# Which queue issues the loads, and when a step turns its tiles: a transformer block on one Trainium2 core

## The chip, the cores and the metric

The kernel runs on one core of one Trainium2 chip. The metric is the device time of one execution in microseconds (us), lower is better. The core has TensorE (PE in the profile: matmuls; PEld: its weight loads), VectorE (DVE), ScalarE (ACT), GpSimd (POOL) and SyncE (SP). Each engine works through its own instruction stream in the order of the program and waits on semaphores. Transfers are issued by an instruction in the stream of SP, ACT or POOL; they are then carried out by 16 DMA engines.

## The reference, cut to what matters

A parallel transformer block over 4 sequences of 512 tokens with 512 features, all in float32: layer norm, causal attention with 16 heads and ALiBi slopes, and a gated feed-forward part whose three 2048 x 512 weight matrices are cubic splines through a few thousand control points.

```python
x = L0_attn_x                                   # (4, 512, 512)
xn = _layernorm(x, axis=-1)
# attention, 16 heads of 32
scores = einsum('bhqd,bhkd->bhqk', q, k) / sqrt(32) + slope[h] * distance[k]
attn = softmax(where(causal, scores, min), axis=-1)
ctx = einsum('bhqk,bhkd->bhqd', attn, v)
# feed-forward, weights interpolated from control points
inter = silu(xn @ gate_w.T) * (xn @ up_w.T)
x = x + ctx @ Wo + bo + inter @ down_w.T
```

## The kernel before, in words

There are two stages. In the first (attention) the normalised x of each batch is turned, projected to q, k and v, and run through softmax; the second (feed-forward) works on few interpolated rows instead of the dense weights. The change lies wholly in the first.

**Units and steps.** Attention is cut into 64 units: 4 batches (b), 4 groups of 4 heads (hg), and 4 query tiles of 128 queries in the order i = 0, 3, 2, 1 (`QUERIES`). Unit i has (i+1)*128 keys. A loop over n issues in step n parts of several units, so each engine's stream is a fixed software pipeline. Before the change, step n issues in this order:

- `swap(n-2)`: DVE turns the unit's probabilities in 32 x 32 blocks (L896, waits for POOL), then SP issues four transfers (L898) that gather the blocks into `moved` (i = 1 to 3, one buffer) or `first` (i = 0);
- `normalize(n-1)`: DVE takes reciprocals of the sums (L878, waits for ACT), POOL multiplies (L880);
- `scores(n)`: PE multiplies q and k into four PSUM banks `s` (L840), DVE adds the ALiBi distance, takes the minimum of the negated score and writes `p` (L851, four instructions, called the minima here);
- `values` in every fourth step (n = 4g+7, for group g): PE multiplies probabilities and v (L914), ACT keeps the result (L929);
- `exponentials(n)`: ACT (L866);
- the spline terms: DVE multiplies and adds tables (L1034) that become the feed-forward weights. A credit decides how many a step gets: `TERMS[n % 4]` is added, each term has a cost. When a term has read its buffer, the next load into that buffer is issued in the same step;
- `items[n]` and `small[n]`: projections (L777, L813), the output projection (L484, with the addition on DVE at L491 and its write `mid` at L494), statistics, and loads.

A unit's `p{i}` has one buffer. So the minima of unit n+4, which has the same i, wait until the four transfers of unit n have read it. `moved` has one buffer too, so the transfers of i = 3 wait until the previous group's `values` have read it. The four `s` banks make `scores(n+1)` wait for the minima of unit n.

**Queues.** Nearly all transfers are issued by SP, in program order with the four of each swap: loads of x (`load_x`, L595), of the tables for the spline terms (L645, L646, L671), of xT for the residual (`proj`'s `load`, L479), of features (`load_feat`, L548), and writes of samples (`keep_samples`, L499 to L503) and moments (`stretch_moments`, L527). POOL issues the copies into `table` (L545).

Of the kernel before, what the change touches and what calls it, by code (L numbers as in the profile page):

```python
# [18 lines left out]
P = 128  # L19
# [4 lines left out]
NB = D // P  # L24
# [5 lines left out]
LAG_SWAP = 2  # L30
# [21 lines left out]

TERMS = (1.4, 0.7, 1.4, 0.7)
NW, NW4 = 11, 4
# [346 lines left out]
def block_kernel(  # L401
# [70 lines left out]

    def proj(b, r, pool, tag):

        xt = []

        def load():
            xt.append(xtp.tile([P, S], F32, name="xt"))
            nc.sync.dma_start(out=xt[0], in_=xT[b, r * P : (r + 1) * P, :])  # L479

        def go():
            ps = pool.tile([P, S], F32, name=tag)
            for c in range(NB):
                nc.tensor.matmul(  # L484
                    ps,
                    lhsT=wsb["o"][:, c, r * P : (r + 1) * P],
                    rhs=ctxT[b][:, c, :],
                    start=(c == 0),
                    stop=(c == NB - 1),
                )  # L490
            nc.vector.scalar_tensor_tensor(  # L491
                xt[0], ps, bocol[:, r : r + 1], xt[0], ALU.add, ALU.add
            )
            nc.sync.dma_start(out=mid[b][:, r], in_=xt[0])  # L494

        return [load, go]

    def keep_samples(b):
        nc.sync.dma_start(  # L499
            out=samples[b][1 : D + 1].rearrange("(c p) s -> p c s", p=P), in_=xnT[b]  # L500
        )
        nc.sync.dma_start(out=samples[b][:1], in_=lone[0][:1])
        nc.sync.dma_start(out=samples[b][D + 1 : D + NW], in_=lone[0][: NW - 1])  # L503

    def stretch_moments(b, pool):
# [15 lines left out]
        for k, ps in enumerate(banks):  # L521
            n = 64 if k == 2 else P
            o = pool.tile([P, S], F32, name="out", bufs=3)
            nc.scalar.copy(o[:n], ps[:n])
            for s, (at, half) in place.items():
                if at == k:
                    nc.sync.dma_start(out=rows[s], in_=o[half * 64 : (half + 1) * 64])  # L527

# [17 lines left out]

    def load_feat(b, q):
        nc.sync.dma_start(out=feat[b][:, q], in_=table[b][:, q])  # L548

# [27 lines left out]
    with ExitStack() as att:  # L577
# [11 lines left out]

        def load_x(b, tiles=range(NB)):  # L590
            if tiles[0] == 0:
                xpt[b] = xpp.tile([P, NB, D], F32, name="xp")
            for t in tiles:
                r = (b * NB + t) * P
                nc.sync.dma_start(out=xpt[b][:, t], in_=xpf[r : r + P, :])  # L595

# [39 lines left out]
        def row_terms():  # L636
# [4 lines left out]

            def load(n):
                c, w = parts[n]
                tab, own = place(n % 2)
                nc.sync.dma_start(out=tab, in_=coef[c])  # L645
                nc.sync.dma_start(out=own, in_=rowpts[c, w])  # L646

            for n, (c, w) in enumerate(parts):
# [6 lines left out]
                if c:  # L655
                    terms.append((1.2, to, to, tmp, ALU.add))
            return [lambda: load(0), lambda: load(1)]

        def down_terms():
# [7 lines left out]
            def load(*steps):  # L667
                for n in steps:
                    for k, source in enumerate((downtab, downpts)):
                        given = source[at[n] : at[n + 1]].rearrange("(p x) -> p x", p=P)  # L670
                        nc.sync.dma_start(out=part(n, k), in_=given)  # L671

            loads[len(terms) - 1] = lambda: load(0, 1, 2)
            for n, (kind, lo, hi, c) in enumerate(DOWN_STEPS):
                to = (dR if kind == "v" else dM)[:, lo:hi].rearrange("p a n -> p (a n)")
# [263 lines left out]
        def project_out(b, spots):  # L939
            for r, n in enumerate(spots):  # L940
                load, go = proj(b, r, ps_m, "mm")
                items[n - 2].append(load)
                items[n].append(go)

        for b in range(B):
# [16 lines left out]
            if b + 1 < B:  # L962
# [8 lines left out]
                if b + 2 < B:  # L971
                    items[at + 11].append(lambda b=b: load_x(b + 2))
        for b in range(B):
# [4 lines left out]
        for q in range(NB):  # L978
            items[54 + NB * q].append(lambda q=q: load_feat(0, q))
        for b in range(B):  # L980
# [30 lines left out]
        for load in first_loads:  # L1011
            load()
        done, credit = 0, 0.0

        for n in range(len(units) + LAG):
            u = units[n] if n < len(units) else None
            if 0 <= n - LAG_SWAP < len(units):
                swap(units[n - LAG_SWAP])
            if 0 <= n - 1 < len(units):
                normalize(units[n - 1])  # L1020
            if u:
                scores(u)
# [248 lines left out]
```

## Time and profile before

| | |
|---|---|
| median of three runs | 556.83 us (554.96 to 560.12) |
| profiled execution, its own time | 559.8 us |
| its span, first to last instruction | 558.0 us |
| mean granted TensorE clock | 0.959 |
| PE busy | 521.5 us, 93% |
| DVE busy | 370.1 us, 66% |
| ACT busy | 259.1 us, 46% |
| POOL busy | 241.3 us, 43% |
| q1 (transfers issued by SP) | 107.78 MB, 65.4% of 16 engines' span |
| q0 (transfers issued by POOL) | 8.40 MB, 5.3% |

The steps of the first stage run from about 25 us to 398 us; the feed-forward stage takes the rest. A busy share of PE counts matmuls with ends that the profile models, so a matmul that is stretched by a wait or by a lower clock counts as busy. The durations below are therefore held against the shortest ones of the same shape. ACT issues no transfer in this profile.

### The profile page before, as it was taken

How to read it: one execution, taken by the hardware profiler on the slowest of the kernel's cores; microseconds unless marked ns; L12 is line 12 of the kernel's file. 1: busy time of each engine (PE TensorE's matmuls, PEld its weight loads, DVE VectorE, ACT ScalarE, POOL GpSimd, SP SyncE). 2: the span in 40 equal slices, each digit the busy share in tenths (PEclk: the TensorE clock that was granted, in tenths of full speed). 3: DMA queues.
4: the chain of work that ended last, by engine and by line, in shares of the span. 5: the costliest groups of instructions: out<-in, count | busy, mean ns of one | idle time of the engine just before them, and what ended most of it. 6: DMA issues, size and time to landing. Idle time of an engine off the chain costs nothing.

```text
span 558.0 us, 11701 instructions
## 1 busy us (share of the span) xinstructions
PE 521.5 (93%) x4012; PEld 246.6 (44%) x4012; DVE 370.1 (66%) x934; ACT 259.1 (46%) x710; POOL 241.3 (43%) x428
## 2 busy tenths in 40 slices
PE   7999999699989989998998999986799899999996
PEld 5633443244444433444443434432335555646552
DVE  5177988559688866878985755683143583665836
ACT  2375567256337526633665654655014322534322
POOL 2032545436345643644566445442068476122310
PEclk9999899899989979998999999898799899899999
DMA  8928678987777788776586478687658667645344
GB/s 317 353 89 241 186 224 234 294 215 187 220 231 217 219 279 224 196 226 173 163 240 170 111 224 216 192 242 198 178 173 256 203 228 260 205 149 202 125 160 160
DMA packets 72060, 116.94 MB, mean 210 GB/s; under 512 B 11104, under 2 KB 35680, under 8 KB 71488
## 3 DMA queue, kind: packets, MB, share of 16 engines
q1 hardware_dynamic: 67392, 107.78, 65.4%
q0 software_dynamic: 4608, 8.40, 5.3%
q8 instruction: 32, 0.52, 0.4%
q14 instruction: 28, 0.23, 0.1%
HBM read 49.56 MB, written 23.68 MB: 131 GB/s over the span
## 4 chain that ended last, share of the span: by engine, by line
PE 67%; DMA 12%; issue 6%; SPq 5%; POOL 4%; DVE 4%; ACT 2%; DVEq 0%; POOLq 0%; ACTq 0%
PE mm L777 15%; PE mm L813 8%; PE g L560 7%; PE s L840 7%; PE mm L484 7%; DMA moved<-p 6%; PE c L914 6%; PE o L1147 6%; SPq L898 5%; PE o L1164 3%; PE o L484 3%; PE o L1093 3%; DMA inner<-made 2%; POOL p L880 2%; DVE p L851 2%
## 5 line engine op out<-in xcount | busy, mean ns | idle before, releaser
L880 POOL TENSOR_SCALAR p<-p,inv 128x128 f32<-128x128 f32 (+3 forms) x256 | 147.3, 587 | 206.4 <-DVE inv L878 193.2
L866 ACT ACTIVATE p<-p,low 128x128 f32<-128x128 f32 (+3 forms) x256 | 140.4, 550 | 77.9 <-DVE low L851 41.8
L896 DVE STREAM_TRANSPOSE p<-p 128x512 f32<-128x512 f32 (+1 forms) x64 | 96.2, 1503 | 18.1 <-POOL p L880 18.1
L851 DVE CUSTOM_DVE_ANT_1 p<-s,dist 128x128 f32<-128x128 f32 (+2 forms) x192 | 69.0, 415 | 31.1 <-PE s L840 20.2
L840 PE MATMUL s<-kT,qT 32*128 32x256 f32 (+3 forms) x512 | 72.6, 480 | 8.3 <-DVE low L851 8.2
L1069 POOL COPY made<-inner 128x512 f32<-128x512 f32 x64 | 38.8, 636 | 88.4 <-DVE inner L1068 55.3
L560 PE MATMUL g<-feat,wT 32*64 32x512 f32 x832 | 65.4, 602 | 0.0
L777 PE MATMUL mm<-xnT,wq 128*128 128x512 f32 (+1 forms) x136 | 62.7, 606 | 0.7 <-ACT v L821 0.7
L813 PE MATMUL mm<-wv,xnT 128*128 128x512 f32 x128 | 60.8, 618 | 1.2 <-ACT xnT L762 1.2
L777 PE MATMUL mm<-xnT,wk 128*128 128x512 f32 (+1 forms) x136 | 59.4, 579 | 0.2 <-ACT xnT L762 0.2
L1061 ACT ACTIVATE act<-g 128x512 f32<-128x512 f32 x60 | 31.0, 604 | 59.7 <-PE g L560 59.6
L914 PE MATMUL c<-moved,v 128*32 128x384 f32 (+2 forms) x512 | 42.4, 482 | 16.4 <-DMA moments<-out 7.4
L840 PEld LDWEIGHTS s<-kT,qT 32*128 32x128 f32 x512 | 32.7, 183 | 56.3 <-DVE low L851 26.1
L851 DVE CUSTOM_DVE_ANT_0 p<-s,dist 128x512 f32<-128x512 f32 x64 | 40.3, 686 | 17.6 <-PE s L840 10.9
L866 ACT ACTIVATION_READ_ACCUMULATOR p<-p,low 128x1 f32 x256 | 47.9, 187 | 0.0
L484 PE MATMUL mm<-ctxT,wo 128*128 128x512 f32 x96 | 45.4, 620 | 0.0
L560 PEld LDWEIGHTS g<-feat,wT 32*64 32x64 f32 x832 | 31.3, 136 | 22.2 <-issue 11.7
L1068 DVE TENSOR_TENSOR inner<-g,act 128x512 f32<-128x512 f32 x40 | 24.8, 684 | 22.4 <-PE g L560 10.7
L777 PEld LDWEIGHTS mm<-xnT,wq 128*128 128x128 f32 x136 | 25.8, 198 | 27.8 <-issue 24.7
L777 PEld LDWEIGHTS mm<-xnT,wk 128*128 128x128 f32 x136 | 24.5, 189 | 30.6 <-issue 24.6
L813 PEld LDWEIGHTS mm<-wv,xnT 128*128 128x128 f32 x128 | 23.6, 194 | 31.2 <-issue 25.5
L1147 PE MATMUL o<-inner,dRM 32*64 32x512 f32 x512 | 36.6, 588 | 0.0
(100 smaller groups left out, 575.3 us busy)
## 6 DMA issues: line engine op xcount, KB each, us to landing
moved<-p SPq DMA_DIRECT2D x64, 256.0 KB
moved<-p SPq DMA_DIRECT2D x64, 192.0 KB
moved<-p SPq DMA_DIRECT2D x64, 128.0 KB
feat<-table SPq DMA_DIRECT2D x16, 512.0 KB
inner<-made SPq DMA_DIRECT2D x32, 256.0 KB
table<-samples POOLq DMA_DIRECT2D x64, 88.0 KB, 3.8
xp<-in_xp_dram SPq DMA_DIRECT2D x16, 256.0 KB
feat<-in_coef_dram SPq DMA_DIRECT2D x8, 512.0 KB
```

Of the source, the lines that this page charges most:

```text
L484: nc.tensor.matmul(ps, lhsT=wsb["o"][:, c, r * P : (r + 1) * P], rhs=ctxT[b][:, c, :], start=(c == 0), stop=(c == NB - 1),)
L560: nc.tensor.matmul(ps[k][cols, :], lhsT=wT[rows, q, 2 * w + part, cols], rhs=feat[b][rows, q, part, :], start=(part == 0), stop=(part == 1),)
L777: nc.tensor.matmul(ps[0][:, tokens], lhsT=wsb[name][:, c, hg * P : (hg + 1) * P], rhs=xnT[b][:, c, tokens], start=(c == 0), stop=(c == NB ...
L813: nc.tensor.matmul(ps[0], lhsT=xnT[b][:, c, t * P : (t + 1) * P], rhs=wsb["v"][:, c, :], start=(c == 0), stop=(c == NB - 1),)
L840: nc.tensor.matmul(ps[j], lhsT=qk[b, hg, "q"][rows, i * P : (i + 1) * P], rhs=keys[rows, :, : i + 1], start=True, stop=True,)
L851: nc.vector.tensor_tensor_reduce(out=p[:, :, :, j], in0=ps[j].rearrange("p (r c y) -> p r c y", r=NB, y=Q32), in1=dist[:, :, NB - 1 - i :] ...
L866: nc.scalar.activation(by_head(p)[:, :, j], by_head(p)[:, :, j], AF.Exp, bias=low[:, j : j + 1], scale=-1.0, accum_out=total[:, j : j + 1],)
L880: nc.gpsimd.tensor_scalar(by_head(p)[:, :, j], by_head(p)[:, :, j], inv[:, j : j + 1], 1.0, ALU.mult, ALU.mult)
L896: nc.vector.transpose(flat, flat)
L914: nc.tensor.matmul(ps[j * HD : (j + 1) * HD, i * P : S if i else P], lhsT=vals[b][:, c, hg * P + j * HD : hg * P + (j + 1) * HD], rhs=w[.. ...
L1069: nc.gpsimd.tensor_copy(made[:, k], four[:, k])
L1147: nc.tensor.matmul(sums[b][r][cols, :], lhsT=dR[rows, a, cols], rhs=o[rows, :], start=(a == 0), stop=False,)
```

## The change

It has three parts. First, the loads of x for batches 2 and 3, the table loads that are issued inside the loop, the xT loads of three batches, the feature loads of batch 0, and all writes of samples and moments are issued in ACT's stream. What is issued ahead of the loop stays with SP, as do the transfers of `swap` and the writes of `mid`. Second, a step now issues `scores` first, then `normalize`, `values`, and then `swap`; only the last tile of a group (i = 1) is still turned ahead of the minima. Third, the table loads are issued one step after the term that frees their buffer (`due`), `TERMS` gives 1.6 in place of 1.4 in even steps, and an empty term of cost 2.4 stands ahead of the terms of the down weights.

```diff
-TERMS = (1.4, 0.7, 1.4, 0.7)
+TERMS = (1.6, 0.7, 1.6, 0.7)
...
-    def proj(b, r, pool, tag):
+    def proj(b, r, pool, tag, queue=nc.sync):
...
-            nc.sync.dma_start(out=xt[0], in_=xT[b, r * P : (r + 1) * P, :])
+            queue.dma_start(out=xt[0], in_=xT[b, r * P : (r + 1) * P, :])
...
     def keep_samples(b):
-        nc.sync.dma_start(
+        nc.scalar.dma_start(
             out=samples[b][1 : D + 1].rearrange("(c p) s -> p c s", p=P), in_=xnT[b]
         )
-        nc.sync.dma_start(out=samples[b][:1], in_=lone[0][:1])
-        nc.sync.dma_start(out=samples[b][D + 1 : D + NW], in_=lone[0][: NW - 1])
+        nc.scalar.dma_start(out=samples[b][:1], in_=lone[0][:1])
+        nc.scalar.dma_start(out=samples[b][D + 1 : D + NW], in_=lone[0][: NW - 1])
...
-                    nc.sync.dma_start(out=rows[s], in_=o[half * 64 : (half + 1) * 64])
+                    nc.scalar.dma_start(out=rows[s], in_=o[half * 64 : (half + 1) * 64])
...
-            def load(n):
+            def load(n, queue=nc.scalar):
                 c, w = parts[n]
                 tab, own = place(n % 2)
-                nc.sync.dma_start(out=tab, in_=coef[c])
-                nc.sync.dma_start(out=own, in_=rowpts[c, w])
+                queue.dma_start(out=tab, in_=coef[c])
+                queue.dma_start(out=own, in_=rowpts[c, w])
...
-            return [lambda: load(0), lambda: load(1)]
+            return [lambda: load(0, nc.sync), lambda: load(1, nc.sync)]
...
-                        nc.sync.dma_start(out=part(n, k), in_=given)
+                        nc.scalar.dma_start(out=part(n, k), in_=given)
...
             loads[len(terms) - 1] = lambda: load(0, 1, 2)
+            terms.append((2.4,))
...
-                load, go = proj(b, r, ps_m, "mm")
+                load, go = proj(b, r, ps_m, "mm", nc.scalar)
...
-                    items[at + 11].append(lambda b=b: load_x(b + 2))
+                    items[at + 11].append(lambda b=b: load_x(b + 2, queue=nc.scalar))
...
-            items[54 + NB * q].append(lambda q=q: load_feat(0, q))
+            items[54 + NB * q].append(lambda q=q: load_feat(0, q, nc.scalar))
...
-        done, credit = 0, 0.0
+        done, credit, late = 0, 0.0, []
...
-            if 0 <= n - LAG_SWAP < len(units):
-                swap(units[n - LAG_SWAP])
+            turned = units[n - LAG_SWAP] if 0 <= n - LAG_SWAP < len(units) else None
+            if turned and turned[2] == QUERIES[-1]:
+                swap(turned)
+            if u:
+                scores(u)
             if 0 <= n - 1 < len(units):
                 normalize(units[n - 1])
-            if u:
-                scores(u)
             if n % NB == NB - 1 and n >= NB + LAG:
                 g = n // NB - 1
                 values(g // NHG, g % NHG)()
+            if turned and turned[2] != QUERIES[-1]:
+                swap(turned)
             if u:
                 exponentials(u, range(NG))
...
-            late = []
+            due, late = late, []
             while done < len(terms) and credit > 0.0:
                 cost, *term = terms[done]
-                nc.vector.tensor_tensor(*term)
+                if term:
+                    nc.vector.tensor_tensor(*term)
                 done += 1
                 credit -= cost
                 if done in loads:
                     late.append(loads[done])
-            for step in (*items[n], *small[n], *late):
+            for step in (*items[n], *small[n], *due):
                 step()
```

More of the change, by code (lines that the diff above doesn't have):

```diff
@@ L545, in copy_rows, with load_feat @@
             nc.gpsimd.dma_start(out=to, in_=rows)
-    def load_feat(b, q):
-        nc.sync.dma_start(out=feat[b][:, q], in_=table[b][:, q])
+    def load_feat(b, q, queue=nc.sync):
+        queue.dma_start(out=feat[b][:, q], in_=table[b][:, q])
     def product(b, q, w, pool, tag):
@@ L588, in block_kernel, with load_x @@
         xpt = {}
-        def load_x(b, tiles=range(NB)):
+        def load_x(b, tiles=range(NB), queue=nc.sync):
             if tiles[0] == 0:
@@ L594, in load_x @@
                 r = (b * NB + t) * P
-                nc.sync.dma_start(out=xpt[b][:, t], in_=xpf[r : r + P, :])
+                queue.dma_start(out=xpt[b][:, t], in_=xpf[r : r + P, :])
         for k in range(2):
```

## The prediction, made before the changed kernel ran

> **What bounds the kernel now.** I read the page first, then busy time by stretches, the timeline of one engine at a time inside the stretches where PE idles, and the waits of DVE. The page:
>
> ```profile
> span 558.0 us, 11701 instructions
> PE 521.5 (93%) x4012; PEld 246.6 (44%) x4012; DVE 370.1 (66%) x934; ACT 259.1 (46%) x710; POOL 241.3 (43%) x428
> ```
>
> PE is the bound, so the time can fall only by what PE idles or is stretched. The stretches show where (columns: busy us and instructions of PE, PEld, DVE, ACT, POOL; granted clock, DMA share, GB/s):
>
> ```profile
> 97.00:114.00 17.00, 11.56 (x66) 4.94 (x67) 9.27 (x23) 4.17 (x12) 6.05 (x10) 0.80 0.90 286
> 149.00:170.00 21.00, 19.44 (x101) 9.05 (x100) 18.27 (x54) 9.68 (x33) 10.93 (x16) 0.92 0.79 250
> 190.00:210.00 20.00, 17.32 (x72) 7.56 (x71) 14.26 (x34) 7.52 (x21) 8.68 (x16) 0.83 0.85 278
> 384.00:398.00 14.00, 5.81 (x47) 2.08 (x44) 1.25 (x1) 3.54 (x7) 0.21 (x1) 0.76 0.88 234
> ```
>
> Idle time stands beside a lower clock: a stop of PE is followed by matmuls at half speed, so a stop costs more than its length. Outside these and the stretches named below PE is busy almost without a gap. The first stretch on SP, DVE and PE:
>
> ```profile
> 88.53 2.46 SPq L595 DMA_DIRECT2D xp<-in_xp_dram  x4
> 92.09 2.79 SPq L898 DMA_DIRECT2D moved<-p  x4
> 95.01 0.56 SPq L499 DMA_DIRECT2D samples<-xnT  x1
> 98.86 5.25 SPq L527 DMA_DIRECT2D moments<-out  x5
> 104.42 2.55 SPq L898 DMA_DIRECT2D moved<-p  x4
> ```
> ```profile
> 91.27 1.25 DVE L896 STREAM_TRANSPOSE p<-p 128x1024 f32<-128x1024 f32 x1 [0.83 <-POOL p L880]
> ```
> ```profile
> 109.37 4.06 PE L914 MATMUL c<-moved,v 128*32 128x384 f32 x32 [4.65 <-DMA moved<-p]
> ```
>
> Unit 11 is turned by 92.5, but its four transfers start to be issued at 104.42, 12 us later: SP still has x, samples and moments ahead of them. PE then stands 4.65 us, and the 32 matmuls take 4.06 us where 2.12 is usual (the same line at 158.44). The second stretch has another cause:
>
> ```profile
> 157.66 0.75 DVE L491 SCALAR_TENSOR_TENSOR xt<-mm,bcol,xt 128x512 f32<-128x512 f32 x1 [1.98 <-PE mm L484]
> 159.38 2.30 DVE L896 STREAM_TRANSPOSE p<-p 128x2048 f32<-128x2048 f32 x1
> 161.67 0.39 DVE L851 CUSTOM_DVE_ANT_1 p<-s,dist 128x256 f32<-128x256 f32 x1
> ```
> ```profile
> 162.13 1.52 PE L840 MATMUL s<-kT,qT 32*128 32x128 f32 x8 [1.56 <-DVE low L851]
> 163.57 5.40 PE L777 MATMUL mm<-xnT,wq 128*128 128x512 f32 x8
> ```
>
> The scores of unit 23 are there at 158.3, but DVE turns unit 21 (2.30 us) before it takes their minima. PE needs the banks back, stops 1.56 us, and the next eight matmuls take 5.40 us in place of 3.70. The stretch from 244 to 265 has the same busy 19.44 and clock 0.92. The waits of DVE, and two of them in time, for later:
>
> ```profile
> DVE p L896 <- POOL p L880: 18.1, 25, 2.0
> DVE p L851 <- DMA moved<-p: 12.1, 6, 4.4
> DVE inv L878 <- ACT p L866: 11.2, 9, 3.6
> ```
> ```profile
> 199.44 0.56 DVE L851 CUSTOM_DVE_ANT_1 p<-s,dist 128x384 f32<-128x384 f32 x1 [4.39 <-DMA moved<-p]
> 348.11 0.69 DVE L851 CUSTOM_DVE_ANT_0 p<-s,dist 128x512 f32<-128x512 f32 x1 [3.29 <-DMA moved<-p]
> ```
>
> **Part one, the queue: what it frees.** 97 to 114: PE idle 17.00 - 11.56 = 5.4, slow matmuls 4.06 - 2.12 = 1.9, scores drawn out to 2.13 at 102.24 where 0.71 is usual: 1.4; together 8.8. 190 to 210 has the same pattern (x at 187.03, samples and tables to 199.8 ahead of the transfers of unit 27, turned by 190.8): idle 2.7 plus 17% of 20 us of clock, 3.4: 6.1. In 280 to 300 PE idles 1.5 behind samples. In 337 to 364 PE idles 1.9 and 6% of 27 us of clock is gone, 1.6; the minima at 348.11 wait for transfers that stood behind moments and features; I take half, 1.8, because these transfers take long by themselves too. In 384 to 398 PE waits 7.4 for the last unit, turned by 385.5 and issued from 387.17: 1.7 can be had, the rest is the tail's own chain. Sum 19.9.
>
> A rule speaks against this part: in the Trainium skill, "DMA: Bandwidth & Descriptors", section "Issuing engines are not separate DMA queues", transfers from all engines run on the same 16 DMA engines, and issuing from several saves only the sequencer's time, "usually small relative to the DMA itself". Here the row shows 12 us of exactly that time, between 92.5 and 104.42, on PE's path. By the rule taken strictly, the queue part would bring nothing and the sum below would end near 556 instead of 536.
>
> **What it costs ACT.** Moved are 8 loads of x (median 0.46), 12 of L645 and L646 (0.46), 24 of L671 (0.46), 12 of xT (0.51), 4 of features (0.58), 20 writes of moments (0.58) and 12 of samples (about 0.6): 92 issues, 47 us, if ACT takes SP's medians. ACT issues none before, so the bounds are SP's shortest (35 us) and longest (124 us) of each line. ACT is busy 253.15 - 52.06 = 201 us of the 373 from 25 to 398, so 47 fit on the whole and the idle 172 hides them; bursts don't. Step 12 gets ten (samples 3, moments 5, a table pair); SP spent 95.0 to 104.1, 9 us, on eight of them. Queued behind on ACT are the exponentials of unit 13 and the projections' evacuations, for which DVE's reciprocals and PE's banks wait. The new order gives about one step (5.5 us, 355 us over 64 steps) of slack, so I charge 4 there and 1 for all other bursts (five issues at step 28, four at 11 and 27, six at 21 and 54): 5, bounds 0 and 20 (two and a half times as long everywhere, by 124 against 47). The fourth xT load of batches 1 and 2 waits on ACT for the write of the first (on SP "mid<-xt" was waited for 5.4 us in three times); behind it stand exponentials that have that step of slack: 0, at most 5. The other moved transfers wait for data that is done a step before: 0. If the slack is gone, ACT's 47 us are the price of rival B.
>
> **Part two, the order.** Minima first: stops like 162.13 go. 149 to 170: 1.56 + (5.40 - 3.70) = 3.3; 244 to 265 the same, 3.3; a stop of this kind near 360 of 0.6. DVE's waits for POOL and ACT (29.3 us) mostly go as well, since turn and reciprocal then stand a step further from what they need; DVE is seldom the last, so I take a tenth, 3. Sum 10.2. No instruction is added. The price: tiles of i = 0, 3, 2 are turned after the minima and reciprocal of the step, 0.9 to 2.0 us later, so their transfers read `p` later while the minima of the unit four on come earlier. For i = 3 the transfers wait for `values` of the same step in any case, which hides most of it. I charge 3; bounds 0 and rival C.
>
> **Part three, the terms.** The same DVE work, 4.6 against 4.2 credits in four steps, 10% denser up to step 46. Only 57 to 79 has DVE near full (20.44 of 22): about four terms of 1.4 us there, 10%: 0.6, taken as 1, bounds 0 and 2. Loads go out a step later and are still three steps ahead of their use: 0. The empty term issues nothing.
>
> **Sum.** 19.9 + 10.2 - 5 - 3 - 1 = 21.1. The profiled execution took 559.8 (span 558.0 and 1.8 around it); 559.8 - 21.1 = 538.7. The median shown is 3.0 lower, so the forecast is 536.
>
> **Rivals.**
>
> A, the full gain: the bursts and later turns hide wholly, 559.8 - 30.1 - 3.0 = 526.7, and 517 if the waits left in 364 to 398 shrink by 10 as well. For it: ACT's 54% idle time. Against: DMA share 0.90 in 97 to 114, so some lateness is bandwidth.
>
> B, ACT takes over SP's lateness: the same waits on full DMA engines hold ACT's stream as they held SP's; the queue part brings 0 and costs its 5: 559.8 - 10.2 + 5 + 4 - 3.0 = 555.6. For it: moments' longest issue is 2.0 us at 99.9. Against: exponentials have a step of slack.
>
> C, the buffer of `p` (the slow side): a wait of the minima for the transfers of the unit four earlier replaces the ones removed. On a free SP, unit 41's were issued from 278.34 and its buffer was free at 286.6: 8.3 us. After the change the turn of i = 3 ends minima 1.4, reciprocal 0.1 and turn 2.3 = 3.8 after the step's minima start, and the next minima of i = 3 are due two steps later: at 5.5 us a step 7.2 remain, at 4.5 a step 5.2. It decides once steps are under 6 us; PE's four banks hide about one microsecond. Priced at 8.3 - 5.2 = 3.1 in 16 groups it is 50 us, which with 30.1 gained gives 559.8 - 30.1 + 50 - 3.0 = 577; at half of the groups, with part one's and three's costs, 559.8 - 30.1 + 25 + 6 - 3.0 = 558, and above that it is slower. For it: 199.44 and 348.11. Against: both waits stood behind late issues of SP.
>
> **How the numbers follow.** Forecast (530 to 548) 0.50, A 0.21, B 0.16, C 0.13. About 1% is what a measurement of this kernel can tell, so faster means below 551.3, slower above 562.4. Faster: 0.50 + 0.21 + 0.03 of B + 0.01 of C = 0.75; same: 0.12 of B; slower: 0.12 of C + 0.01 of B = 0.13. The range leaves out the better end of A and the worse of C: 517 to 557.
>
> **What would show it.** Right: the transfers of unit 11 issued within 3 us of its turn; PE's stops at `values` of the third and seventh group gone; no 1.56 us stop behind L491; clock above 0.97 in the first stage; tail stop still over 5 us. Wrong, towards B: the exponentials idle behind ACT's issues and DVE's reciprocals wait for ACT. Towards C: DVE's wait of the minima for "moved" well above 12.1 us.

## The result, and the profile after

The changed kernel takes 582.09 us (median of four runs, 579.05 to 589.41) against 556.4 for the kernel before in the same session: ratio 1.043, 95% interval 1.035 to 1.051. The forecast was 536, with a range from 517 to 557. Its profiled execution took 580.91 us, its span is 579.1, and the mean granted clock is 0.935 in place of 0.959. Ratios here leave disturbed executions out, so that a ratio can differ from the quotient of two medians. All of the loss lies in attention: from the first minima of one batch to those of the next (of the last batch, to the end of its minima) the four batches took 91.3, 95.5, 89.5 and 76.2 us before, and take 93.6, 98.5, 104.5 and 77.6 now; what comes after them is unchanged (179.3 and 179.8).

The page of the changed kernel (busy us and share of the span of each engine):

```profile
span 579.1 us, 11648 instructions
PE 533.5 (92%) x4012; PEld 249.1 (43%) x4012; DVE 370.5 (64%) x934; ACT 257.7 (45%) x710; POOL 237.4 (41%) x428
```

No engine has more to do. PE's 12 extra busy us are matmuls stretched by a lower clock or a wait. The same stretches as before, and the new place of the tail stop (busy of PE, PEld, DVE, ACT, POOL; clock, DMA share, GB/s):

```profile
97.00:114.00 17.00, 14.20 (x82) 5.77 (x82) 8.38 (x24) 7.36 (x19) 5.20 (x8) 0.90 0.89 270
149.00:170.00 21.00, 21.00 (x106) 9.08 (x105) 16.49 (x48) 7.57 (x24) 7.77 (x13) 1.00 0.83 262
401.00:420.00 19.00, 9.75 (x92) 3.22 (x88) 4.37 (x4) 7.64 (x17) 3.00 (x7) 0.77 0.82 208
```

So both stretches on which the forecast rested did improve: from 11.56 to 14.20 busy us at a clock of 0.90 in place of 0.80, and from 19.44 to a full 21.00 at 1.00. PE's stop at the tail, 7.4 us before, is 9.2 now (in the third line). Unit 11, whose transfers were issued 12 us after its turn, in the timelines of DVE, SP and PE:

```profile
93.48 1.23 DVE L897 STREAM_TRANSPOSE p<-p 128x1024 f32<-128x1024 f32 x1
```
```profile
96.22 4.15 SPq L899 DMA_DIRECT2D moved<-p  x4
```
```profile
111.57 2.12 PE L915 MATMUL c<-moved,v 128*32 128x384 f32 x32
```

The turn ends at 94.7. The group of four SP issues around it begins at 96.22 with the last of the tile before; unit 11's own begin at 96.9, 2.2 us after its turn. The matmuls of `values` start without a stop and take their 2.12 us. What was aimed at was hit; the time went elsewhere. The waits of DVE, and PE's longest (total us, times, longest us), first before, then in the changed kernel:

```profile
DVE p L851 <- PE s L840: 31.1, 16, 11.7
```
```profile
PE s L840 <- DVE low L851: 8.2, 8, 1.6
```
```profile
DVE p L852 <- PE s L841: 60.5, 24, 11.7
DVE p L852 <- DMA moved<-p: 20.1, 7, 6.2
DVE inv L879 <- ACT p L867: 11.3, 6, 2.9
```
```profile
PE s L841 <- DVE low L852: 21.7, 11, 5.6
```

The minima waited 31.1 us for scores before, and 60.5 now; for "moved" 12.1, and 20.1 now; PE waited 8.2 us for the minima, and 21.7 now. One such place lies in the third batch, which lost 15 of the 21 us between the two profiled executions. Timelines of DVE, SP, ACT and PE:

```profile
290.29 2.28 DVE L897 STREAM_TRANSPOSE p<-p 128x2048 f32<-128x2048 f32 x1
...
304.71 0.69 DVE L852 CUSTOM_DVE_ANT_0 p<-s,dist 128x512 f32<-128x512 f32 x1 [6.25 <-DMA moved<-p]
```
```profile
292.63 4.32 SPq L899 DMA_DIRECT2D moved<-p  x4
```
```profile
295.20 0.38 ACTq L499 DMA_DIRECT2D samples<-xnT  x1
...
305.01 0.25 ACTq L502 DMA_DIRECT2D samples<-lone  x1
305.49 0.32 ACTq L503 DMA_DIRECT2D samples<-lone  x1
306.07 0.72 ACT L867 ACTIVATE p<-p,low 128x512 f32<-128x512 f32 x1 [10.05 <-DVE low L852]
```
```profile
305.47 3.47 PE L841 MATMUL s<-kT,qT 32*128 32x384 f32 x8 [5.61 <-DVE low L852]
```

Unit 41 (i = 3) is turned from 290.29 to 292.6, after the minima and the reciprocal of its step; its transfers are issued from 292.63, and ACT adds a 1 MB write of samples at 295.20. The minima of unit 45, which need the same buffer `p3`, start at 304.71, 12 us after the turn: the last of the four transfers, issued at 295.24, lands only at 304.4, 9.2 us later. PE stands 5.61 us for its banks and is slow after it (3.47 us for eight matmuls that take 0.93 elsewhere, at 106.20). And ACT, which issued the first write at 295.20, issues the second only at 305.01. Two things come together here, a late turn and a second queue; the experiments try to take them apart.

### The profile page after: what moved, and what is told of

It reads as the page before. It is cut to its first block, busy times and chain, and to the rows that moved or that the text cites. A ratio compares the mean times of both kernels' runs of the same rounds, so it can differ in the third digit from the quotient of the medians.

```text
span 579.1 us, 11648 instructions
## 1 busy us (share of the span) xinstructions
PE 533.5 (92%) x4012; PEld 249.1 (43%) x4012; DVE 370.5 (64%) x934; ACT 257.7 (45%) x710; POOL 237.4 (41%) x428
## 4 chain that ended last, share of the span: by engine, by line
PE 56%; DMA 18%; DVE 10%; SPq 5%; issue 4%; ACT 2%; POOL 2%; ACTq 1%; DVEq 0%; POOLq 0%
DMA moved<-p 12%; PE mm L814 9%; PE mm L778 9%; PE s L841 8%; PE g L560 7%; PE o L1152 5%; SPq L899 5%; DVE p L897 4%; DVE p L852 4%; PE c L915 3%; PE mm L484 3%; PE o L484 3%; PE o L1169 3%; PE o L1098 2%; DMA inner<-made 2%
## 5 line engine op out<-in xcount | busy, mean ns | idle before, releaser
L881 POOL TENSOR_SCALAR p<-p,inv 128x128 f32<-128x128 f32 (+3 forms) x256 | 143.4, 572 | 233.3 <-DVE inv L879 195.9
L841 PE MATMUL s<-kT,qT 32*128 32x256 f32 (+3 forms) x512 | 80.6, 510 | 21.8 <-DVE low L852 21.7
L814 PE MATMUL mm<-wv,xnT 128*128 128x512 f32 x128 | 69.0, 688 | 1.1 <-ACT xnT L763 1.1
L841 PEld LDWEIGHTS s<-kT,qT 32*128 32x128 f32 x512 | 36.0, 193 | 71.7 <-DVE low L852 41.2
L852 DVE CUSTOM_DVE_ANT_0 p<-s,dist 128x512 f32<-128x512 f32 x64 | 40.3, 685 | 36.6 <-DMA moved<-p 20.1
L560 PE MATMUL g<-feat,wT 32*64 32x512 f32 x832 | 61.7, 591 | 0.0
L778 PE MATMUL mm<-xnT,wq 128*128 128x512 f32 (+1 forms) x136 | 59.3, 579 | 0.3 <-DMA wq<-in_Wqp_dram 0.3
L915 PE MATMUL c<-moved,v 128*32 128x384 f32 (+2 forms) x512 | 39.5, 456 | 9.8 <-DMA moments<-out 9.2
L814 PEld LDWEIGHTS mm<-wv,xnT 128*128 128x128 f32 x128 | 27.0, 222 | 37.3 <-issue 30.9
L1073 DVE TENSOR_TENSOR inner<-g,act 128x512 f32<-128x512 f32 x40 | 24.8, 683 | 21.7 <-PE g L560 10.7
L560 PEld LDWEIGHTS g<-feat,wT 32*64 32x64 f32 x832 | 28.5, 131 | 21.5 <-issue 10.9
L545 POOL DMA_DIRECT2D table<-samples x64 | 36.4, 579 | 0.0
```

The lines of the kernel that those rows point to most:

```text
L545: nc.gpsimd.dma_start(out=to, in_=rows)
L560: nc.tensor.matmul(ps[k][cols, :], lhsT=wT[rows, q, 2 * w + part, cols], rhs=feat[b][rows, q, part, :], start=(part == 0), stop=(part == 1),)
L778: nc.tensor.matmul(ps[0][:, tokens], lhsT=wsb[name][:, c, hg * P : (hg + 1) * P], rhs=xnT[b][:, c, tokens], start=(c == 0), stop=(c == NB ...
L814: nc.tensor.matmul(ps[0], lhsT=xnT[b][:, c, t * P : (t + 1) * P], rhs=wsb["v"][:, c, :], start=(c == 0), stop=(c == NB - 1),)
L841: nc.tensor.matmul(ps[j], lhsT=qk[b, hg, "q"][rows, i * P : (i + 1) * P], rhs=keys[rows, :, : i + 1], start=True, stop=True,)
L852: nc.vector.tensor_tensor_reduce(out=p[:, :, :, j], in0=ps[j].rearrange("p (r c y) -> p r c y", r=NB, y=Q32), in1=dist[:, :, NB - 1 - i :] ...
```

## The experiments

The kernel before had a median between 556.4 and 558.5 in all sessions. Medians are in us; ratios with their 95% intervals are against the kernel before in the same session.

### Each part by itself

**The queue part** in the old order, with part three (edit against the changed kernel):

```diff
-if turned and turned[2] == QUERIES[-1]:
+if turned:                     # all four tiles, at the head of the step
     swap(turned)
-scores(u)
 normalize(units[n - 1])
+scores(u)
 values(...)
-if turned and turned[2] != QUERIES[-1]:
-    swap(turned)
```

> Parts one and three alone: the loads and writes are issued by ACT, the terms are as in the changed kernel, but a step turns its tile and takes the reciprocal ahead of the scores, as before. Theory T1 (the later turn costs: the minima of i = 3 wait for transfers out of a single buffer of p): this kernel is not slower than before, 535 to 557 us, and its wait of the minima for moved stays at or under 12 us. Theory T2 (the queue costs: ACT is held behind transfers of SP and the two queues share the DMA engines): slower than before, 565 to 580 us, with most of the 25 us lost here.

Measured: 572.18, ratio 1.023 (1.016 to 1.029), as T2 had it.

**The order alone**, all transfers with SP, the old terms:

```diff
-swap(units[n - LAG_SWAP])
+if turned and turned[2] == QUERIES[-1]: swap(turned)
+scores(u)
 normalize(units[n - 1])
-scores(u)
 values(...)
+if turned and turned[2] != QUERIES[-1]: swap(turned)
```

> Part two alone: minima first and only the last tile of a group turned ahead, all loads in SP's queue and the terms as before. T1: slower than before, 570 to 585 us, with the wait of the minima for moved over 20 us. T2: 545 to 557 us, since the stops of PE behind the output projection go and nothing is added.

Measured: 575.48, ratio 1.032 (1.024 to 1.040), as T1 had it. So each theory is right about its part.

**Part three alone**, on SP in the old order:

```diff
-TERMS = (1.4, 0.7, 1.4, 0.7)
+TERMS = (1.6, 0.7, 1.6, 0.7)
...
-for step in (*items[n], *small[n], *late):
+for step in (*items[n], *small[n], *due):
```

> Part three alone: TERMS, the empty term and the loads one step later, everything issued by SP in the order of before. If the terms cost nothing, within 1% of before, 553 to 561 us. If the denser terms are a part of what the queue alone loses, 562 us or more.

Measured: 557.63, ratio 1.003 (0.998 to 1.007): it costs nothing.

Each of the two large parts is slower by itself, by about 13 and 18 us by the ratios, and together by 24. That the whole is less than the sum is not shown: the intervals are too wide for it.

### The order: where its loss comes from

The waits of DVE with the order alone:

```profile
DVE p L851 <- PE s L840: 53.4, 21, 11.3
DVE p L851 <- DMA moved<-p: 38.0, 16, 6.0
...
DVE p L896 <- POOL p L880: 1.9, 5, 0.7
```

The wait of the turn for POOL fell from 18.1 to 1.9 us, as the prediction wanted. It came back in the first two lines: 31.1 to 53.4 for scores, 12.1 to 38.0 for "moved". From a unit's last minimum to the end of its turn there passed 8.8, 8.8 and 8.9 us (means over the 16 units each of i = 0, 3 and 2) before, and 13.4, 11.6 and 12.4 with the new order.

**A second buffer for `p3`** in the changed kernel, and in the order alone; room for it was made by allocating and loading `edge` and `basist` after attention:

```diff
-p = sp.tile([P, NB, i + 1, NG, Q32], F32, name=f"p{i}")
+p = sp.tile([P, NB, i + 1, NG, Q32], F32, name=f"p{i}", bufs=2 if i == 3 else 1)
```

> The changed kernel with two buffers for the p of i = 3, so that the minima of i = 3 no longer wait for the transfers of the unit four earlier. To make room, edge and basist are made and loaded after the attention stage. T1: the stops of PE at the scores after i = 3 go, 20 us or more are won back, 545 to 562 us. T2: at most 5 us are won back, 575 to 583 us.

> Part two alone (the order, all loads in SP) with two buffers for the p of i = 3, edge and basist made after the attention stage. T1 (the later turn costs through the one buffer of p): the 18 us that the order alone lost come back, 545 to 560 us, and the wait of the minima for moved falls from 38 us to under 15 us. Rival (the later turn costs because the transfers into moved come late for values): 568 to 577 us as in the order alone.

Measured: 567.81 (ratio 1.014, 1.004 to 1.023) for the changed kernel, 14 us less than without it; 566.22 (1.020, 1.013 to 1.027) for the order alone, 9 us less (these two intervals still overlap). Both win back less than T1 had, and the wait for "moved" in the order alone did not fall under 15 us. The control, the same second buffer in the kernel before:

> The kernel before with two buffers for the p of i = 3 and edge and basist made late, as a control: its minima waited 12 us in all for moved, 3.3 us of it seen by PE near 348, so 552 to 558 us. If it falls much more, the second buffer's gain in the other kernels is not the price of the order.

Measured: 556.94, ratio 1.001 (0.998 to 1.004). The buffer is worth nothing where the turn is early and 9 to 14 us where it is late, so waiting for the single buffer is a real part of the loss, about half by the medians. With it no minima of i = 3 wait for "moved" any longer in the order alone (22.2 us without it), but the other buffers stayed single, and the wait moved there: those of i = 2 wait 30.6 us in place of 9.7, those of i = 1 9.4 in place of 6.0, 40.0 in all. How the rest of the loss divides was not tried.

**Turning i = 3 ahead as well** in the changed kernel:

```diff
-if turned and turned[2] == QUERIES[-1]:
+if turned and turned[2] in (1, 3):
...
-if turned and turned[2] != QUERIES[-1]:
+if turned and turned[2] not in (1, 3):
```

> The changed kernel, but tiles of i = 3 are turned ahead of the minima as well, as i = 1 is; only i = 0 and 2 are turned late. T1: the transfers of i = 3 still wait for the values of the same step, so they start about a microsecond earlier; 8 to 20 us won back, 560 to 574 us. T2: no change, 578 to 584 us.

Measured: 572.65, ratio 1.023 (1.015 to 1.030), 9.4 us back, from the other side: the transfers come earlier instead of having a second buffer, and the minima wait 13.4 us for "moved" in place of 20.1. This run alone does not show the buffer, since ACT's idle time ahead of its issues, of which more below, fell as well, from 29.2 to 15.6 us.

**Is it the turn, or the reciprocal ahead of it?** Both stand behind the wait for scores in the new order. I took the reciprocal to be the root. First the changed kernel with `normalize` put back ahead of `scores`:

```diff
-scores(u)
 normalize(units[n - 1])
+scores(u)
```

> The changed kernel, with normalize put back ahead of scores; the turn of i = 0, 3 and 2 stays behind the minima. Theory, the reciprocal stands in DVE's stream behind the wait for the scores and makes POOL's product and with it the turn late: exponentials' end to reciprocal falls from 7.5 us to about 2.5 for i = 0, minima to turn from 12 to 14 us to about 10 to 11, and of the 25 us lost a third to a half comes back: 566 to 574. Rival, the lateness comes from the turn alone, which still stands behind the minima: 578 to 584. Rival, ACT's waits set the time: 578 to 584 as well, with ACT's idle time ahead of its issues at 25 to 35 us.

Measured: 586.55, ratio 1.051 (1.041 to 1.061). My theory fell. In its trace (an execution of 591.0 us) the reciprocal of i = 0 comes 2.7 us after the exponentials in place of 7.5, and the product right after; but the turn then stands 7.9 us behind the product, and from minima to turn there are 14.4 us as before. And the reciprocal now holds DVE up for ACT:

```profile
DVE inv L879 <- ACT p L867: 49.1, 31, 7.5
```

Then the other half, in the kernel before: every turn at the head of its step, `scores` ahead of `normalize`, all on SP:

```diff
 swap(turned)
-normalize(units[n - 1])
 scores(u)
+normalize(units[n - 1])
```

> The kernel before with one move: scores ahead of normalize, while every turn stays at the head of its step; all transfers stay with SP. Theory after the run with the reciprocal first: what costs is the turn's place behind the wait for the scores, so this one keeps its turns in time (minima to turn 8 to 10 us) and takes 552 to 562. Rival, the reciprocal's place behind that wait delays product and turn by itself: minima to turn 11 to 13 us and 566 to 576, near the 575 of the whole new order on SP.

Measured: 580.25, ratio 1.043 (1.037 to 1.048). My second theory fell too: with the turn in its old place the loss is as large. Minima to turn is 9.2, 10.4 and 11.7 us, between the two, and the waits show another mechanism:

```profile
DVE p L896 <- POOL p L880: 98.3, 57, 2.8
```

The reciprocal of unit n-1 now stands after the minima of n. POOL's four products follow it (some 600 ns each), and the next thing of weight on DVE is their turn: DVE stands 1.7 us in 57 of 64 steps. In the order before, the minima of n lie between a reciprocal and the turn of its product, and cover it. So in the orders tried neither the reciprocal nor the turn could go behind the wait for scores: the first leaves the product without cover, the second makes the transfers late. Of these orders only the one before keeps both ahead.

### The queue: where its loss comes from

The trace shows eight completion semaphores, dealt in turn and in program order to all transfers of SP and ACT. Before each issue in ACT's stream I took the idle time of the issuing sequencer, and looked at what was raised last. In the queue part alone ACT idled 33.8 us ahead of 16 of its 92 issues, each time until the semaphore that the transfer itself signals had been raised by its previous user; in 31.4 of the 33.8 us that was a swap's transfer, issued by SP. The kernel before has the same wait in SP's own stream, but only 2.5 us of it in attention, the longest 1.3 us at 97.56 (a sample row, until a table load issued at 91.09 had landed). The issues themselves took 48.8 us, near the 47 of the prediction. Timelines of ACT in that kernel, and the wait of DVE's reciprocals for it (11.2 us before):

```profile
196.88 0.40 ACT L867 ACTIVATE p<-p,low 128x128 f32<-128x128 f32 x1 [6.27 <-DMA moved<-p]
...
207.15 0.72 ACT L867 ACTIVATE p<-p,low 128x512 f32<-128x512 f32 x1 [7.96 <-DMA samples<-lone]
```
```profile
DVE inv L879 <- ACT p L867: 35.7, 14, 8.3
```

The exponentials stand idle behind loads of x (until 196.88) and of samples and tables (until 207.15): "towards B" in the prediction's terms.

**The same 92 issues on POOL** (`nc.gpsimd` for `nc.scalar`), which in the trace has semaphores of its own:

> Like the queue alone (order as before, terms as in the change), but POOL issues the moved loads and writes in place of ACT. POOL's transfers signal semaphores of their own, which no transfer of SP uses. Theory S (on ACT each issue waits until the transfer of SP that used its semaphore last has landed: 34 us of ACT idle ahead of its issues in the run with the queue alone): this wait is gone, and the time is 540 to 557 us, at or under before, POOL's 92 issues of 0.58 us costing some. Theory R (two rings share the DMA engines, so the transfers of the turned tiles are slower whoever issues the loads): 566 to 575 us, as with ACT.

Measured: 572.39, ratio 1.030 (1.024 to 1.037), no better than ACT. By its numbers theory S fell and theory R came out. No issue waits for a transfer of SP any longer (one waits 4.8 us for POOL's own 1 MB write). The swaps' transfers are slower: from issue to landing they take 5.0 us on the mean, 4.3 with ACT and 4.0 before, and 44 of 256 take over 7 us, 12 with ACT and 8 before. But POOL also stands in the same chain with its products: the turn's wait for them rises from 18.1 to 28.6 us (longest 5.5), and PE's stop at the tail is 12.0 us in place of 7.4. So the run neither shows nor rules out that ACT's waits at the semaphores cost what ACT's kernel loses; it shows that without them a second queue can lose as much.

**The issues split by what they carry**, old order, part three. The 36 table loads alone on ACT:

```diff
 def load(n, queue=nc.scalar): ...                  # tables: ACT
-nc.scalar.dma_start(out=samples[b]..., )
+nc.sync.dma_start(out=samples[b]..., )             # and x, moments, xT, features: SP
```

> The old order of a step with part three, and of the loads only the table loads (36 issues) in ACT's stream; x, samples, moments, xT and features stay with SP. Theory, ACT waits at its issues for landings of the turned tiles: with all 92 issues on ACT its idle time ahead of issues was 33.8 us, of which 12.8 lay at table loads, so ACT idles 9 to 16 us ahead of its issues here, the exponentials are late less often, and the time is 557 to 564, at most half of the 15 us lost with all of them. Rival, it is the length of the issues in ACT's stream: 36 of 92 issues, 40% of the loss, 563. Rival, transfers of two rings that share the 16 DMA engines slow the turned tiles down, whichever engine issues: the tables are 16 of 27 MB, 60% of the loss, 566. A gain below 551 would say that the tables alone are what SP should be freed of.

Measured: ratio 0.992 (0.986 to 0.998), but this rests on two of its ten times (550.4 and 553.3); the median of all ten is 561.18 against 556.44. I read it as open between 4 us gained and 5 us lost. ACT idles 12.3 us ahead of its issues, as the theory had it. The 36 loads are 13 of the 27 MB by the trace's sizes, and not 16, so the rival of the shared engines should have had half of the loss for each half of the issues.

The other 56, with the tables on SP:

> The other half: x, samples, moments, xT and features (56 issues) in ACT's stream, the table loads with SP, old order, part three. Theory, ACT waits for landings: 21.0 of the 33.8 us lay at these lines, the longest at x (3.7) and at the write of the first sample row (7.8), so ACT idles 17 to 25 us ahead of its issues and the time is 564 to 571. Rival, the length of the issues: 60% of the loss, 566. Rival, sharing of the DMA engines by two rings: 11 of 27 MB, 40% of the loss, 563. If both halves come out near 557, the loss needs both and is not a sum over issues.

Measured: 575.22, ratio 1.036 (1.028 to 1.045): at least as much as the whole queue part lost, and more than any of the three theories had. ACT idles 33.8 us ahead of its issues, more than the 17 to 25 that I had worked out from the other trace.

**The same two kernels with loads issued ahead of the swap**, so that a semaphore's previous user would lie further back: x and samples of the 56, then x, samples and tables of the 92:

```diff
+for step in ahead[n]:      # load_x, keep_samples (second kernel: and the table loads)
+    step()
 swap(turned)
```

> As the run with x, samples, moments, xT and features in ACT's stream (575.2), but the loads of x and the writes of samples of batches 1 to 3 are issued at the head of their step, ahead of the swap, in place of at its end. Theory, ACT's issue waits for the last transfer on the same semaphore: of 33.8 us of ACT's idle time ahead of its issues 32 lay at these two lines; with the swap's transfers of the same step behind them it falls to 5 to 15 us, DVE's wait of the reciprocal for the exponentials falls from 36 to under 22 us, and the time to 556 to 566. Rival, the issues' own length or the bytes in a second ring: nothing of that changes, 571 to 579.

> The queue part whole (92 issues on ACT, old order of a step, 572.2), with x, samples and the table loads at the head of their step, ahead of the swap. Theory, the wait for the semaphore: ACT's idle time ahead of its issues falls from 33.8 to 5 to 15 us and the time to 553 to 563. Rival, length or bytes: 568 to 576. If ACT's idle time falls and the time does not, the wait is not what costs.

Measured: 571.53 (1.028, 1.022 to 1.033) and 582.8 (1.047, 1.040 to 1.053). The edit didn't do what it was for: ACT still idles 30.2 and 31.4 us, most of it at the small sample rows, since the user eight transfers back was then a transfer of the previous swap, still on its way. The second kernel is even 10 us slower than the same 92 issues at the end of a step, perhaps because ACT now stands still ahead of the step's exponentials and no longer after them. They leave the question where it was.

**Split by where ACT waited.** Of the 56, the 40 at which it hardly waited (the 1 MB writes of samples, the moments, xT, features: 12 of 14 MB) on ACT, then only the 16 at which it did (x and the small sample rows):

```diff
 # first kernel                                  # second kernel: the other way round
 nc.scalar.dma_start(out=samples[b][1 : D + 1]...)
-nc.scalar.dma_start(out=samples[b][:1], ...)
+nc.sync.dma_start(out=samples[b][:1], ...)
-load_x(b + 2, queue=nc.scalar)
+load_x(b + 2)
```

> Of the 56 issues on ACT in the run of 575.2 us, 40 stay there (the 1 MB writes of samples, moments, xT, features: 12 of 14 MB); the 8 loads of x and the 8 writes of the small sample rows, at which ACT waited 32 of 33.8 us, go back to SP. Old order, part three. Theory, the wait for the semaphore: ACT idles 2 to 7 us ahead of its issues, DVE's reciprocals wait for the exponentials under 16 us in place of 36, and the time is 554 to 563. Rival, length of the issues or bytes in a second ring: about three quarters of the 19 us lost remain, 567 to 573.

> The complement: only the 8 loads of x and the 8 writes of the small sample rows are issued by ACT, 16 issues and 2 of 14 MB; all else is with SP. Old order, part three. Theory, the wait for the semaphore: ACT idles 22 to 34 us ahead of its issues, DVE's reciprocals wait for the exponentials 24 to 36 us, and most of the 19 us is lost, 566 to 576. Rival, length or bytes: 16 issues of half a microsecond, 557 to 562.

Measured: 559.9 (ratio 1.007, 1.003 to 1.012) with 40 issues, and 552.43 (0.988, 0.984 to 0.992) with 16. DVE's wait of the reciprocals for the exponentials, in the 56, the 40 and the 16:

```profile
DVE inv L879 <- ACT p L867: 36.0, 11, 10.8
```
```profile
DVE inv L879 <- ACT p L867: 16.4, 9, 7.6
```
```profile
DVE inv L879 <- ACT p L867: 11.4, 10, 3.2
```

The first came out as the theory of the wait has it: three quarters of the issues and most of the bytes, 4.0 us of idle time, and a loss of 0.7%. The swaps' transfers took nearly as long in it as with the 56 (4.2 and 4.3 us from issue to landing on the mean, 4.0 before), while ACT's idle time and the loss fell: this speaks for the wait, and against the transfers' mean time. The second run did not come out so: the 16 issues alone wait only 11.4 us, and the kernel gains 1.2%. Apart the two halves cost 0.7% and gain 1.2%; together they cost 3.6%. The trace of the 56 shows how, at the writes of samples for the last batch (ACT's timeline):

```profile
294.25 0.42 ACTq L499 DMA_DIRECT2D samples<-xnT  x1
...
303.90 0.25 ACTq L502 DMA_DIRECT2D samples<-lone  x1
304.21 0.42 ACTq L503 DMA_DIRECT2D samples<-lone  x1
304.83 0.72 ACT L867 ACTIVATE p<-p,low 128x512 f32<-128x512 f32 x1 [8.93 <-DMA moved<-p]
```

The write at 303.90 signals the semaphore that a swap's transfer, issued by SP at 294.18, signalled before it. That one landed 9.7 us after its issue, beside the 1 MB write that ACT had issued at 294.25; with the 16 alone, where SP issues the 1 MB write behind the swap, the same transfer of the same unit (issued at 275.58) landed after 5.9 us, and the one that ACT's issue waited for there (issued at 271.90) after 6.2. Meanwhile the minima of the next unit are done from 299.4 on, and its exponentials start at 304.83, 5.4 us late. By this place it takes both: a long transfer in another queue that makes the swap's transfers slow, and an issue of ACT behind it that has to wait for one of them.

The Trainium skill, "DMA: Bandwidth & Descriptors", section "Queues, rings and completion order", says that each DMA engine takes turns, packet by packet, between the queues that have work for it. The 9.7 and 5.9 us agree with a swap that shares the engines with the 1 MB write, though no run here shows the turns themselves.

All kernels with loads on ACT: idle time ahead of its issues, DVE's wait of the reciprocals for ACT, and the ratio.

| on ACT, order | issues | ACT idle, us | DVE for ACT, us | ratio |
|---|---|---|---|---|
| x and sample rows, old | 16 | 11.4 | 11.4 | 0.988 |
| tables ahead, x spread, old | 36 | 11.0 | 7.3 | 0.991 |
| tables, old | 36 | 12.3 | 9.4 | 0.992 (medians of all: 1.009) |
| all but x, rows, tables, old | 40 | 4.0 | 16.4 | 1.007 |
| all but tables, ahead, old | 56 | 30.2 | 31.2 | 1.028 |
| all but tables, old | 56 | 33.8 | 36.0 | 1.036 |
| all, old | 92 | 33.8 | 35.7 | 1.023 |
| all, ahead, old | 92 | 31.4 | 39.3 | 1.047 |
| all, changed kernel | 92 | 29.2 | 11.3 | 1.043 |

With up to some 12 us of idle time at most about 1% is lost; with about 30 the old order loses 2.3% to 4.7%. The number of issues and their length do not sort the rows (40 lose little, 56 more than 92). No run took the wait away and left all transfers as they were, so that the slow transfers' own share stays open.

The last row differs: in the changed kernel DVE waits for ACT no more than in the kernel before (11.3 and 11.2 us), though ACT idles 29.2 us ahead of its issues. At the place in the third batch the exponentials could start at 305.4, when the first minima are done, and start at 306.07; ACT's stand from 295.6 on costs 0.7 us there. What the queue adds at this place shows in the transfers instead: those of unit 41 take 11.8 us from the first issue to the last landing, and 8.0 both before and with the order alone, where the third batch takes 94.3 us in place of 104.5. So the hold of ACT is seen as a wait of DVE in the old order alone; in the changed kernel, where DVE is late by itself, it is not.

### What SP's bursts were worth

All on SP, old order; the loads of x one in each of four steps, the moments of batch 1 four steps later:

```diff
-items[at + 11].append(lambda b=b: load_x(b + 2))
+for t in range(NB):
+    items[at + 11 + t].append(lambda b=b, t=t: load_x(b + 2, range(t, t + 1)))
...
-items[(5, 12, 54, 65)[b]].append(...)
+items[(5, 16, 54, 65)[b]].append(...)
```

> The kernel before, all on SP in the old order, with the bursts in SP's stream spread: one load of x in each of the steps at+11 to at+14 in place of four in one, and the moments of batch 1 at step 16 in place of 12. If the 12 us between turn and issue of unit 11 and its stop at the values were SP's burst, as the prediction read them, the stop of 4.65 us goes and the time falls by up to the 14.9 us that the prediction gave to those two stretches: 542 to 551. If the DMA engines' bandwidth is what makes the turned tiles late there, spreading moves the wait and the time stays at 554 to 560.

Measured: 552.72, ratio 0.994 (0.990 to 0.998), between the two expectations. In the profiled executions PE's stop at `values` is 2.2 us in place of 4.65. The first batch takes 84.5 us in place of 91.3: 6.8, against the 8.8 that the prediction gave to this place. The second takes 98.4 in place of 95.5 and gives 2.9 back. What a burst costs is there, but not all of the gain is kept. Joined with the tables on ACT, issued ahead of the swap, and the terms of part three:

> The kernel before with the table loads alone in ACT's stream, at the head of the step after the term that frees their buffer, the loads of x spread over four steps on SP and the moments of batch 1 at step 16. Theory: the two gains that showed, of 3 us (spread) and between nothing and 4 (tables), add up to 546 to 554. Rival: both free the same wait of the turned tiles for SP, 551 to 556. Slower than 558 would say that ACT's 36 issues cost at other places.

Measured: 552.37, ratio 0.991 (0.988 to 0.995). This and the 16 issues (552.43) are, with the spread loads alone (552.72), the best versions found, 0.6% to 1.2% faster than the kernel before.

## Why the prediction was wrong, step by step

**What bounds the kernel, and the stops named:** right. The stops at `values` of unit 11's group and behind L491 are gone, and the matmuls there take their usual times. The clock did not come out: above 0.97 was forecast for the first stage, and it fell there from 0.95 to 0.92; PE has new stops, its waits for the minima above all (8.2 us before, 21.7 now).

**The queue frees 19.9: mis-sized.** No version that frees SP gained more than 7 us, the 1.2% of the 16 issues. Each stop was priced as if the time after it kept the gain; the run with spread loads shows 6.8 freed and 2.9 taken back in the next batch. The 12 us of unit 11 were also not only "exactly that time" of SP's issuing: SP itself stood in them, 1.3 us at 97.56 until an earlier load had landed. That the transfers share the same DMA engines wherever they are issued is the rule of the Trainium skill which the prediction weighed ("Issuing engines are not separate DMA queues"). The measured gain lies much nearer to its "usually small" than to 19.9, but the rule, read as "nothing gained", would have given 556, and the queue part took 572. It was to bring 13.9 us net (19.9 less 5 for ACT and 1 for the terms) and lost about 13.

**ACT's cost of 5: the failed step.** The 47 us of issues were right (48.8, and 45.7 in the changed kernel) and did hide. What the sum lacked is a wait at the issue itself. The sentence "the other moved transfers wait for data that is done a step before: 0" looked for waits on data; the trace of before, where SP issues all, has only 2.5 us of the other kind. With 33.8 us of it in the queue part alone, and 13 us lost there after a gain of at most 7, I estimate the price at 13 to 20 us in place of 5, slower transfers of the swaps included; how it divides between the two is open. Rival B named the symptom, idle exponentials, but priced it at no more than ACT's own issues: 555.6. In the changed kernel the symptom is absent (DVE waits 11.3 us for ACT, 11.2 before), and the queue's cost shows as later landings of the swaps.

**The order frees 10.2: right where it looked.** The stop is gone and the 18.1 us of DVE's waits for POOL are 1.9 with the order alone. They were not free to take, though: DVE now waits for scores instead (31.1 us before, 53.4 with the order alone). The order was to bring 7.2 us net of its price of 3, and lost 18.

**Later turns 3: the other failed step.** "0.9 to 2.0 us later" counted the instructions put ahead of the turn and not the wait in their midst: DVE works in program order, so the turn also waits for `scores(n)`. From the last minimum it ends 2.8 to 4.6 us later with the order alone, 3.2 to 5.4 in the changed kernel. Rival C, its direction and its sign were right: the minima do wait for the transfers of the unit four before, DVE's wait for "moved" rose from 12.1 to 20.1 (38.0 with the order alone), and a second `p3` takes back 9 to 14 us by the medians, so this step alone measured at least three times its price. "Against: both waits stood behind late issues of SP" and the argument that `values` hides most of it were the wrong weights. The measured 582 lies even above the 577 at which rival C ended, since C left the queue's gain whole. Its 0.13 was too low.

**Terms 1:** right; 0.6 measured, within the error.

## What to carry to other kernels

Before moving an instruction behind another in an engine's stream, ask what that other waits for: the move costs the wait as well as its duration, and it is paid again wherever a single buffer closes the loop. A transfer put into a compute engine's stream held that engine at the issue here, for a completion semaphore shared with the other queue, so count what else is on its way at that moment and not only the issues. Gains added up from single stops were an upper bound here (6.8 us freed at one place, 2.9 of them lost in the next batch); test one with the smallest edit (here, spreading four loads) before adding them up.

## What was unexpected of the hardware and its queues

Issues in two streams are coupled: ACT, free otherwise, stood 9.4 us at one small write (from 295.6 to 305.0) until a transfer of SP's had landed. And a single 1 MB write in a second queue went with 9.7 us from issue to landing for a swap's transfer beside it, against 5.9 for the same transfer with the write behind the swap. With 16 issues in ACT's stream the kernel gained 1.2%, with 56 it lost 3.6%.
